# A selective-scan network on one core: the loads of delta * u in a different split and order

## The chip, the cores and the metric

The kernel runs on one core of one Trainium2 chip. The time is device microseconds of one execution, from three runs, of which the median counts. One further execution was taken by the hardware profiler; every row, wait and timeline below comes from it.

## What is computed

The network has four layers over a batch of 4 images of 64 x 64 pixels and 96 channels. Layers 0 and 1 are selective-scan (Mamba) layers and take most of the time; layers 2 and 3 are linear attention with a small quantised feed-forward part. A scan layer expands to 192 channels, applies a 3 x 3 convolution, and runs a state-space recurrence along four directions of the image (rows, columns, and both reversed). Its core, for every image, direction, channel and 16 states, over 4096 positions, is

```
dA = exp(delta * A)
h  = dA * h + delta * u * B        # u: the convolved input
y  = sum over the 16 states of h * C
```

after which the four directions are added, normalised, gated and projected.

## The kernel before

The two scan layers work on the images in pairs, so there are four phases (2 layers x 2 pairs). A phase first prepares (`prepare`): normalisation, convolution, `delta`, and the product `delta * u`, which go to DRAM; the end of the previous phase (`finish`) is woven into it. Then comes the scan stage (`scan_phase`), which is written out by hand, with the order of every engine's instructions fixed.

In the scan stage the 128 partitions hold 8 groups (4 directions x 2 images) x 16 states. Of these, partition p belongs to group (p / 4) mod 8, so each quarter of 32 partitions holds all 8 groups with 4 of the states. The work is cut into 128 units: 8 chunks of 512 positions, and in each chunk 16 blocks of 12 channels. One unit is a tile `h` of 128 partitions x 12 channels x 512 positions, f32. For each unit:

- SP loads the tile `dlt` (delta in three bf16 parts, 24 partitions, line 376), and into `h` the product `delta * u` (line 396). DRAM holds that product for the 8 groups, in two equal copies; each row of it goes to four partitions.
- GpSimd multiplies `h` by B in place, three channels at a time (`times_b`, line 406), half a unit ahead of the scans.
- TensorE spreads `dlt` over the partitions into PSUM (`replicate`, line 412), ScalarE makes `exp` of it (`decay`, line 416), and VectorE does the recurrence, one scan of 512 positions for each channel (`scan`, line 423). From chunk 1 on the scans start from the carry of the chunk before.
- One unit later TensorE multiplies by C (`contract`, line 441), ScalarE evicts (line 453), and SP stores `y` in four transfers (line 461).

There are four `h` buffers. `load(units[at + 3])` is written after the last scan of unit `at` and after the stores of unit `at - 1`, and so three units ahead; a chunk's B and C are loaded by four transfers each at the ends of blocks 8 and 15. All these transfers are in SP's queue in that order. The transfers in SP's queue use eight completion semaphores in turn, so each one waits until the eighth-last has landed.

`load_quarters(u, e, n, first, quarters)` loads `n` channels from channel `e` into `quarters` quarters from quarter `first` on: 32 partitions from one copy of `delta * u`, or 64 partitions from both. One packet is one partition's 6 channels, 12,288 bytes. The order in which `load` calls it is a tuple and an inner loop over the two halves of the channels:

```
        n = EB // 2
        for first, quarters in ((1, 2), (0, 1), (3, 1)):
            for e in range(0, EB, n):
                self.load_quarters(u, e, n, first, quarters)
```

Of the kernel before, what the change touches and what calls it, by code (L numbers as in the profile page):

```python
# [32 lines left out]
EB = 12  # L33
# [47 lines left out]
class Consts:  # L81
# [3 lines left out]
    def load(self, pool, name, shape):  # L85
        t = pool.tile(shape, F32, name=name)
        self.nc.sync.dma_start(t, self.a[name])
        return t
# [39 lines left out]
class Scans:  # L128
# [19 lines left out]
    def prepare(self, ph):  # L148
# [16 lines left out]
        with self.tc.tile_pool(name="prep", bufs=1) as wp, self.tc.tile_pool(  # L165
# [3 lines left out]
            def load(name, shape, at=0):  # L169
                t = wp.tile([at + shape[0]] + shape[1:], F32, name=name)  # L170
                nc.sync.dma_start(t[at:], a[pre + name])
                return t

            xp = load("x_proj", [C, 2, 2, XD2])
            dt_w = load("dt_w", [XD2 - 2 * NS, 2, E], at=2 * NS)
            conv_b = load("conv_b", [C, 2])
            ds = load("Ds", [C, 2, K])
            dsum = wp.tile([C, 2], F32, name="dsum")
# [202 lines left out]
    def load(self, u):  # L381

        nc, ph = self.nc, u.ph
        u.h = self.units.tile([128, EB, TC], F32, name="h", bufs=4)
        self.load_delta(u)
        n = EB // 2
        for first, quarters in ((1, 2), (0, 1), (3, 1)):
            for e in range(0, EB, n):
                self.load_quarters(u, e, n, first, quarters)

    def load_quarters(self, u, e, n, first, quarters):

# [591 lines left out]
```

## Time and profile before

| | us |
|---|---|
| median of three runs (lowest, highest) | 12483.71 (12462.94, 12492.15) |
| the profiled execution's own time | 12443.48 |
| its span, first to last instruction | 12441.7 |
| scan stages, four | 1909, 1911, 1912, 1929 |
| before the first scan; the three preparations between the stages; after the last scan | 774; 923, 932, 926; 1201 |
| busy: TensorE, VectorE, GpSimd, ScalarE | 10107.0, 9376.9, 7386.0, 7185.6 |
| loads of `h`: transfers, size | 2048 of 384 KB (32 partitions), 1024 of 768 KB (64 partitions) |

PE is TensorE's matmuls, PEld its weight loads, DVE VectorE, ACT ScalarE, POOL GpSimd, SP SyncE; a q after the name is that engine's queue. A row of the page gives the line, engine, operation, tiles (out<-in), shape and count, then busy time and mean ns of one, then the engine's idle time before it and what ended most of it. Rows of digits are tenths of busy time in 40 equal slices of the span. The row of DMA is the mean over 16 DMA engines: 0.5 there can mean that eight of them are full. Timeline rows give the start, the length, and in brackets the idle time before and what ended it.

### The profile page before, as it was taken

Reading aid. Unit: us, or ns where it says so; the run is one execution under the profiler, and the core shown is the slowest. Engines: PE = TensorE matmul, PEld = TensorE weight load, DVE = VectorE, ACT = ScalarE, POOL = GpSimd, SP = SyncE. Lnnn points to the kernel's source line nnn. Section 1 sums busy time; section 2 is a strip of 40 time slices with the busy share of each in tenths; the row PEclk is TensorE's granted clock in tenths of the full one; section 3 lists DMA queues with packets and bytes.
Section 4 is the critical chain, followed back from the end, with each engine's and each line's share of the span. In section 5 each row is a group of like instructions: output and inputs, shape, how many; then the busy total and the mean of one; then the engine's idle time right before and its main releaser. Section 6 shows DMA issues by size and latency. Waiting matters only on the chain.

```text
span 12441.7 us, 340858 instructions
## 1 busy us (share of the span) xinstructions
PE 10107.0 (81%) x147008; PEld 4972.1 (40%) x147008; DVE 9376.9 (75%) x9235; ACT 7185.6 (58%) x11815; POOL 7386.0 (59%) x2316
## 2 busy tenths in 40 slices
PE   7758888879878888879878888888878888887777
PEld 2224444433334444433334444443334444444333
DVE  2479999963569999982469999992459999993567
ACT  2456666644456666653456666663446666662556
POOL 0159999950149998960139899880129989990000
PEclk8665565669675555659775656558776655557787
DMA  3567676754667676764566777664567666663110
GB/s 92 172 227 247 244 248 247 248 168 140 213 205 246 245 247 244 250 200 128 176 215 244 246 247 249 243 226 125 174 202 249 244 243 245 245 244 122 30 21 11
DMA packets 882704, 2491.45 MB, mean 200 GB/s; under 512 B 279058, under 2 KB 561840, under 8 KB 737456
## 3 DMA queue, kind: packets, MB, share of 16 engines
q1 hardware_dynamic: 552496, 2163.38, 50.6%
q10 hardware_dynamic: 328704, 306.26, 8.5%
q8 instruction: 1158, 18.97, 0.7%
q14 instruction: 346, 2.83, 0.1%
HBM read 1955.42 MB, written 513.80 MB: 198 GB/s over the span
## 4 chain that ended last, share of the span: by engine, by line
DMA 53%; PE 20%; SPq 8%; DVE 7%; ACT 4%; issue 4%; POOL 3%; ACTq 1%; POOLq 0%; DVEq 0%
DMA h<-du 47%; PE c L260 8%; SPq L396 7%; POOL h L406 3%; PE f L591 2%; DVE h L423 2%; PE d L306 2%; DMA yk<-y 1%; PE c L289 1%; PE f L600 1%; POOL parts L320 1%; PE f L682 1%; DMA du<-du_sb 1%; PE y L441 1%; DVE parts L321 1%
## 5 line engine op out<-in xcount | busy, mean ns | idle before, releaser
L406 POOL TENSOR_TENSOR h<-h,b 128x1536 f32<-128x1536 f32 x2048 | 7016.6, 3456 | 780.6 <-DMA h<-du 369.0
L423 DVE TENSOR_TENSOR_SCAN h<-a,carry,h 128x512 f32<-128x512 f32 x5376 | 6356.7, 1259 | 391.8 <-POOL h L406 360.9
L416 ACT ACTIVATE a<-a,a_col 128x512 f32<-128x512 f32 x6144 | 4030.3, 662 | 1966.6 <-PE a L412 1814.4
L441 PEld LDWEIGHTS y<-h,cw 128*32 128x32 f32 x131072 | 2886.3, 145 | 3597.6 <-issue 1606.1
L441 PE MATMUL y<-h,cw 128*32 128x48 f32 x131072 | 3702.1, 269 | 438.0 <-ACT a L416 216.9
L412 PE MATMUL a<-dlt,rep 24*128 24x512 bf16 x6144 | 3319.4, 551 | 884.8 <-DVE h L423 782.1
L320 POOL CAST parts<-dl 96x1024 bf16<-96x1024 f32 x256 | 341.3, 1348 | 3092.1 <-DVE dl L317 2785.6
L316 DVE TENSOR_TENSOR du_sb<-dl,xc 96x1024 f32<-96x1024 f32 x256 | 397.3, 1577 | 1296.2 <-ACT dl L314 1234.8
L453 ACT COPY d<-y 128x384 f32<-128x384 f32 x2048 | 979.6, 478 | 485.7 <-PE y L441 432.7
L260 PE MATMUL c<-xn,taps 96*96 96x512 f32 x2304 | 1034.1, 609 | 73.5 <-DVE xn L245 71.0
L423 DVE TENSOR_TENSOR_SCAN h<-a,h 128x512 f32<-128x512 f32 x768 | 869.6, 1201 | 189.0 <-ACT a L416 110.6
L412 PEld LDWEIGHTS <-rep 24*128 24x128 bf16 x6144 | 471.9, 101 | 903.6 <-issue 451.0
L306 PE MATMUL d<-xd,dt_w 7*96 7x512 f32 x1024 | 520.8, 859 | 254.9 <-ACT xd L292 225.6
L260 PEld LDWEIGHTS c<-xn,taps 96*96 96x96 f32 x2304 | 382.6, 167 | 707.5 <-issue 628.7
L823 POOL MEMSET tn<- 1x4096 f32 x8 | 27.8, 3506 | 865.0 <-PE pa L843 514.7
L267 ACT ACTIVATE xc<-c,conv_b 96x512 f32<-96x512 f32 x128 | 87.3, 682 | 718.1 <-PE c L260 633.2
L591 PE MATMUL f<-yk,perm 128*128 128x384 f32 x1024 | 415.9, 546 | 99.6 <-DMA yk<-y 88.8
L314 ACT ACTIVATE dl<-d 96x1024 f32<-96x1024 f32 x256 | 252.0, 1017 | 400.9 <-DMA delta<-parts 234.5
L321 DVE TENSOR_TENSOR parts<-dl,parts 96x1024 bf16<-96x1024 f32 x256 | 366.9, 1455 | 153.2 <-POOL parts L320 153.1
L289 PE MATMUL c<-xc,x_proj 96*103 96x512 f32 x512 | 420.2, 958 | 4.2 <-ACT xc L267 4.2
L306 PEld LDWEIGHTS d<-xd,dt_w 7*96 7x96 f32 x1024 | 151.7, 212 | 542.4 <-ACT xd L292 295.8
L360 ACT ACTIVATE cw<-c,gmask 128x256 f32<-128x256 f32 x512 | 287.9, 573 | 126.2 <-DMA h<-du 65.9
(114 smaller groups left out, 5650.6 us busy)
## 6 DMA issues: line engine op xcount, KB each, us to landing
h<-du SPq DMA_DIRECT2D x1024, 768.0 KB
h<-du SPq DMA_DIRECT2D x2048, 384.0 KB
delta<-parts ACTq DMA_DIRECT2D x512, 288.0 KB
dlt<-delta SPq DMA_DIRECT2D x512, 288.0 KB
du<-du_sb SPq DMA_DIRECT2D x256, 384.0 KB
du<-du_sb ACTq DMA_DIRECT2D x256, 384.0 KB
y<-d SPq DMA_DIRECT2D x2048, 48.0 KB
yk<-y SPq DMA_DIRECT2D x256, 384.0 KB
```

Of the source, the lines that this page charges most:

```text
L260: nc.tensor.matmul(rows(ps[:C]), taps[:, tap, h * C : (h + 1) * C], xn[:, ROWS * c + dy : ROWS * (c + 1) + dy, dx : dx + HW], start=tap == ...
L289: nc.tensor.matmul(rows(ps[:XD2]), xp[:, k, h], u[:, h], start=h == 0, stop=h == 1)
L306: nc.tensor.matmul(ps[:, m], dt_w[part, k, m * C : (m + 1) * C], xd[part], start=True, stop=True)
L321: nc.vector.tensor_tensor(parts[:, 2], delta, parts[:, 1], ALU.subtract)
L396: self.nc.sync.dma_start(u.h[32 * first : 32 * (first + quarters), e : e + n].rearrange("p e t -> p (e t)"), source.rearrange("a g e t -> ...
L406: self.nc.gpsimd.tensor_tensor(h, h, b, ALU.mult)
L412: self.nc.tensor.matmul(u.a[n], rep, u.dl[:, n], start=True, stop=True)
L416: self.nc.scalar.activation(u.a[n], u.a[n], AF.Exp, scale=u.ph.a_col[:, at : at + 1])
L423: self.nc.vector.tensor_tensor_scan(u.h[:, n], u.a.pop(n), u.h[:, n], 0.0 if u.c == 0 else u.ph.carry[:, at : at + 1], ALU.mult, ALU.add,)
L441: self.nc.tensor.matmul(view(u.y[32 * j : 32 * j + 32], l2 * EB, (8 * EB, 4), (1, EB)), u.ph.cw[u.c][:, l1, 8 * j + l2], view(u.h, 64 * l1 ...
L453: self.nc.scalar.copy(u.d[:, :, :, l1], u.y[:, : 32 * EB].rearrange("p (t h x) -> p t h x", t=4, h=2))
L591: nc.tensor.matmul(ps[:, : 4 * C].rearrange("p (w v e) -> p w v e", w=4, v=nv), cst.perm[:, k], view(t, off, (sw if k < 2 else -sw, 4), (1 ...
```

## The change

The three kinds of transfer, each made for channels 0 to 5 and for channels 6 to 11, were the middle half (partitions 32 to 95), quarter 0 (0 to 31) and quarter 3 (96 to 127): six transfers. Channels 6 to 11 keep these three. Channels 0 to 5 come in two halves instead: 64 to 127 and 0 to 63. The order is now

1. channels 6 to 11, partitions 32 to 95
2. channels 6 to 11, partitions 0 to 31
3. channels 0 to 5, partitions 64 to 127
4. channels 0 to 5, partitions 0 to 63
5. channels 6 to 11, partitions 96 to 127

`load_quarters`, the data and the rest of the kernel are unchanged.

```diff
--- before.py
+++ after.py
@@ -384,9 +384,8 @@
         u.h = self.units.tile([128, EB, TC], F32, name="h", bufs=4)
         self.load_delta(u)
         n = EB // 2
-        for first, quarters in ((1, 2), (0, 1), (3, 1)):
-            for e in range(0, EB, n):
-                self.load_quarters(u, e, n, first, quarters)
+        for first, quarters, e in ((1, 2, n), (0, 1, n), (2, 2, 0), (0, 2, 0), (3, 1, n)):
+            self.load_quarters(u, e, n, first, quarters)
 
     def load_quarters(self, u, e, n, first, quarters):
 
```

## The prediction

> **What bounds the kernel now.** I read the page first, then the busy times by stage, then the waits and the timeline of one unit, then the records of single transfers. From the page:
>
> ```profile
> span 12441.7 us, 340858 instructions
> ...
> DVE  2479999963569999982469999992459999993567
> ...
> DMA  3567676754667676764566777664567666663110
> ...
> DMA 53%; PE 20%; SPq 8%; DVE 7%; ACT 4%; issue 4%; POOL 3%; ACTq 1%; POOLq 0%; DVEq 0%
> ...
> L406 POOL TENSOR_TENSOR h<-h,b 128x1536 f32<-128x1536 f32 x2048 | 7016.6, 3456 | 780.6 <-DMA h<-du 369.0
> L423 DVE TENSOR_TENSOR_SCAN h<-a,carry,h 128x512 f32<-128x512 f32 x5376 | 6356.7, 1259 | 391.8 <-POOL h L406 360.9
> ```
>
> VectorE shows four plateaus of nines, the scan stages. There it is nearly full, and what idle time it has ends with GpSimd's multiply, which itself waits for `h<-du`. The DMA row stands at 6 to 7 tenths, and yet DMA leads the chain. The stages, with columns PE, PEld, DVE, ACT, POOL busy, clock, DMA share, GB/s:
>
> ```profile
> 775.00:2684.00 1909.00, 1621.64 (x34042) 832.57 (x34041) 1805.52 (x1536) 1305.54 (x2268) 1740.52 (x508) 0.60 0.70 245
> 3613.00:5524.00 1911.00, 1624.24 (x34042) 833.32 (x34041) 1806.32 (x1536) 1306.72 (x2269) 1740.56 (x509) 0.60 0.70 244
> 6462.00:8374.00 1912.00, 1625.12 (x34042) 832.86 (x34041) 1806.35 (x1536) 1307.18 (x2268) 1740.75 (x508) 0.60 0.70 244
> 9306.00:11235.00 1929.00, 1626.64 (x34042) 833.21 (x34041) 1807.04 (x1536) 1308.57 (x2268) 1740.52 (x508) 0.60 0.69 242
> ```
>
> Stage time less VectorE busy is 103.5 + 104.7 + 105.7 + 122.0 = 436 us: all that faster loads can give while VectorE does the same scans. Where it sits, from the timeline (VectorE, then GpSimd):
>
> ```profile
> 1510.77 4.78 DVE L423 TENSOR_TENSOR_SCAN h<-a,carry,h 128x512 f32<-128x512 f32 x4
> 1519.54 14.21 DVE L423 TENSOR_TENSOR_SCAN h<-a,carry,h 128x512 f32<-128x512 f32 x12 [3.98 <-POOL h L406]
> ```
>
> ```profile
> 1516.06 13.66 POOL L406 TENSOR_TENSOR h<-h,b 128x1536 f32<-128x1536 f32 x4 [4.48 <-DMA h<-du]
> ```
>
> A unit's twelve scans run without a gap; the stall stands before the first. From the scan starts: scans 1 to 11 of a unit follow each other at 1.177 us (chunks 1 to 7), scan 0 follows after 2.07. A unit takes 15.05 us where VectorE needs 12 x 1.177 = 14.12.
>
> **Why DMA bounds at 0.70.** A 64-partition load is written by 16 engines, four packets of 12,288 B each; a 32-partition load by eight. The trace shows this in the completion counts: the 64-partition load issued at 1513.73 has eight engines landing at 1519.3 to 1519.6 and the other eight at 1521.4 to 1522.8, and every 32-partition load has only eight late completions. So one half of the engines, 0 to 7, has six blocks of four packets a unit, and the other two. Busy times around the stall:
>
> ```profile
> 1516.50:1520.50 4.00, 1.54 (x41) 0.91 (x34) 0.96 (x1) 1.14 (x2) 4.00 (x2) 0.50 1.04 273
> 1520.50:1521.50 1.00, 0.58 (x1) 0.10 (x1) 1.00 (x2) 0.01 (x1) 1.00 (x1) 0.50 0.77 315
> 1521.50:1529.50 8.00, 7.04 (x135) 3.28 (x134) 8.00 (x8) 5.61 (x10) 8.00 (x3) 0.50 0.55 221
> ```
>
> From 1521.5 on half of the engines work, at 221 GB/s, each packet in 0.46 us. In the first stretch all sixteen work and bring only 273 GB/s: packets take 0.6 to 0.95 us there, on both halves. At 1521, again with sixteen at work, packets take 0.46 to 0.47. So two halves can run at full pace or slow each other down, depending on what they write. Engines 0 to 7 never rest: their unit is 6 blocks x 1.85 us (landings 1540.0, 1541.8, 1543.7) = 11.1, the delta tile 1.56, the four y stores 1.2, sum 13.9; the rest of the 15.05, 1.1 us, is lost while both halves are active.
>
> [...]
>
> **The change part by part.** It issues five loads for six: 4 x 128 = 512 units, 512 fewer issues of 0.645 us on SP's queue, which is not on the path once it stops waiting for its eighth-last transfer; 0. Bytes stay. Blocks on engines 0 to 7 go from 6 to 5, on 8 to 15 from 2 to 3. So engines 0 to 7 need 5 x 1.85 + 1.56 + 1.2 = 12.0 us a unit, plus a loss c while both halves work. VectorE's 14.12 is reached at c = 2.1, today's 15.05 at c = 3.05.
>
> No row shows c, so both ends: 0[...]; 3 x 1.85 = 5.55 if each block of engines 8 to 15 collides in full. By today's rate (1.1 us for two blocks) three cost 1.65. By hand from the issue order: engines 0 to 7 spend about 1.5 us on the delta tile first, so they lag not one block but 1.75. Engines 8 to 15 then do halves 32-95, 64-127, 0-63 at 0.7, 2.5, 4.4 us[...]. With some loss beside the delta tile c is 1.1 to 1.8. I take 1.65: 13.65 us, under VectorE's 14.12. GpSimd needs four multiplies at 3.41 us start to start = 13.66; TensorE in three channels 3 x 0.53 + 2 x 0.84 = 3.27 of 3.53 us at clock 0.50, and units without a stall already run so. VectorE becomes the bound.
>
> Order: channels 0 to 5 are complete after the fourth load instead of the fifth[...]. A load is issued at the end of the unit three before its own, and GpSimd must start on it some 24 us later, so about 9 us of lead covers the 4 to 5 us that eight small loads of b and c add in a chunk, as long as a unit's DMA work stays under 14.12; without that cover the stalls return.
>
> Sum: of 436 us, chunk 0 keeps about 3 us a stage, since GpSimd (13.66) is slower there than the scans without carry (12 x 1.128 = 13.54) and starts level: 12. Because the margin is only 0.5 us a unit I leave a tenth of the rest, 40. Saved: 436 - 12 - 40 = 384. The profiled execution, 12443.5 with 1.8 outside its span, would be 12060; the median of the runs is 40 above it, 12483.7, so 12483.7 - 384 = 12100.
>
> **Rivals.**
> Partial gain: c is 2.1 to 3.05, engines 0 to 7 still bound. For: 1.65 is near 2.1, and a backlog makes the next middle half meet the last quarter, as today. Against: the hand schedule. At 14.6 us a unit, 448 units x 0.45 = 200 saved: 12280.
> Slower: the halves fall into step, so that two of engines 8 to 15's blocks collide in full (c = 3.7, beyond the 3.05 where it decides). A unit takes 15.7 us: 448 x 0.65 + 64 x (15.7 - 14.1) = 290 + 100, 12870. For: packets on both halves already double in places, and a transfer waits for the eighth-last one, which ties both halves together. Against: the extra 1.85 us block that is gone, and the packets at 0.46 with sixteen engines.
> Hidden anyway, no change: would need c at 3.05 by chance, or SP's issue as the bound; against the latter, SP waits for loads 502 us of the first scan stage.
> The 64-partition loads not spreading over 16 engines is excluded: they have the shape of today's.
>
> **How the numbers follow.** VectorE bound, 12100, 12030 to 12160: 0.64. Partial, up to 12455: 0.22. Within 0.2% (25 us, about what a measurement of this kernel can tell from no change): 0.04. Slower: 0.10. The low end is the ceiling, 12483.7 - 436, with the runs' spread of 20; up to 12330 takes in most of the partial cases.
>
> **What would show it.** Right: scan stages of 1810 to 1825 us, VectorE busy still 1806; scan 0 following at under 1.4 us; the `h<-du` wait of GpSimd nearly gone; SP waiting for compute more than for transfers; late completions 16, 8, 16, 16, 8 a unit. DMA share stays near 0.7 with GB/s near 258. Wrong: packets near 0.92 us with sixteen engines most of the time, and stages of 1900 or more.

## The result: 4.5% slower

The changed kernel takes 13026.23 us (median of 4 runs, 12980.17 to 13108.25) against 12480.49 of the kernel before beside it: a ratio of 1.0446, 95% interval 1.039 to 1.0501. The forecast was 12100 us, with a range of 12030 to 12330. The profiled execution has a span of 13009.0 us against 12441.7.

The page of the changed kernel, the lines that answer to those shown of before (line numbers are one lower from here on, since the diff takes a line away):

```profile
span 13009.0 us, 339405 instructions
...
DVE  2478888872568888882468988883458898884566
...
DMA  3578888864678878874568878884568888885110
...
DMA 57%; PE 20%; DVE 7%; SPq 6%; ACT 4%; issue 3%; POOL 3%; ACTq 1%; POOLq 0%; DVEq 0%
...
L405 POOL TENSOR_TENSOR h<-h,b 128x1536 f32<-128x1536 f32 x2048 | 7010.6, 3454 | 1359.6 <-DMA h<-du 786.5
L422 DVE TENSOR_TENSOR_SCAN h<-a,carry,h 128x512 f32<-128x512 f32 x5376 | 6361.9, 1260 | 889.0 <-POOL h L405 851.6
```

The work is the same, 3454 ns a multiply and 1260 ns a scan. What grew is the chain of waits that bounded before: GpSimd for the loads (369 to 787 us), VectorE for GpSimd (361 to 852). DMA engines are busier, mostly 8 tenths for 6 to 7. By stage (PE, PEld, DVE, ACT, POOL busy, clock, DMA share, GB/s):

```profile
775.00:2857.00 2082.00, 1668.34 (x34042) 846.47 (x34041) 1808.33 (x1537) 1312.91 (x2269) 1738.54 (x508) 0.55 0.81 225
3790.00:5821.00 2031.00, 1635.16 (x34042) 842.83 (x34041) 1807.21 (x1536) 1300.10 (x2268) 1739.75 (x508) 0.59 0.81 230
6752.00:8809.00 2057.00, 1673.72 (x34088) 848.31 (x34090) 1807.71 (x1536) 1311.33 (x2265) 1739.05 (x508) 0.55 0.81 227
9739.00:11804.00 2065.00, 1658.99 (x34042) 845.47 (x34041) 1806.74 (x1536) 1307.72 (x2268) 1738.93 (x508) 0.56 0.81 226
```

The four stages together are 574 us longer (8235 against 7661), which is all of the span's 567; preparations and tail are as before. VectorE's busy time has not moved. The DMA engines are busy for a larger share (0.81 for 0.70) and move less in that time (227 GB/s for 244): the same bytes at a slower pace. In the transfer records a packet of 12,288 B takes 0.70 us on average, 0.55 before; 36% take over 0.8 us, 9% before. A unit takes 15.9 to 16.7 us in chunks 1 to 7 (means by chunk over the four stages), and the stall sits where it sat, before scan 0 (first row VectorE, second GpSimd):

```profile
4223.26 14.21 DVE L422 TENSOR_TENSOR_SCAN h<-a,carry,h 128x512 f32<-128x512 f32 x12 [2.81 <-POOL h L405]
```

```profile
4219.77 13.65 POOL L405 TENSOR_TENSOR h<-h,b 128x1536 f32<-128x1536 f32 x4 [3.36 <-DMA h<-du]
```

Why packets are slow shows in six microseconds of that unit, with all sixteen engines busy:

```profile
4225.00:4231.00 6.00, 5.21 (x102) 2.45 (x100) 6.00 (x6) 3.91 (x7) 6.00 (x3) 0.50 1.02 232
```

A share of 1.02 and 232 GB/s is little more than what eight engines brought alone in the kernel before (221). In the same stretch the completion counts of the third load (64 to 127) show all sixteen engines landing together, from 4227.96 to 4229.38 but for one straggler at 4233.86, and the fourth (0 to 63) likewise from 4231.47 to 4232.87, with one at 4237.19. All do the same transfer at the same time, into one half of the partitions; packets there take 0.91 us in the median. The planned distance, one half of the engines a block ahead of the other, is not there.

### The profile page after: what moved, and what is told of

Its sections match the earlier page's. It is cut to its first block, busy times and chain, and to the rows that moved or that the text cites. A ratio compares the mean times of both kernels' runs of the same rounds, so it can differ in the third digit from the quotient of the medians.

```text
span 13009.0 us, 339405 instructions
## 1 busy us (share of the span) xinstructions
PE 10247.0 (79%) x147008; PEld 5025.3 (39%) x147008; DVE 9382.0 (72%) x9235; ACT 7191.8 (55%) x11815; POOL 7380.9 (57%) x2316
## 4 chain that ended last, share of the span: by engine, by line
DMA 57%; PE 20%; DVE 7%; SPq 6%; ACT 4%; issue 3%; POOL 3%; ACTq 1%; POOLq 0%; DVEq 0%
DMA h<-du 52%; PE c L260 8%; SPq L395 5%; DVE h L422 3%; POOL h L405 2%; PE f L590 2%; PE d L306 2%; DMA yk<-y 1%; PE y L440 1%; PE c L289 1%; PE f L599 1%; PE f L670 1%; POOL parts L320 1%; DMA delta<-parts 1%; PE f L681 1%
## 5 line engine op out<-in xcount | busy, mean ns | idle before, releaser
L405 POOL TENSOR_TENSOR h<-h,b 128x1536 f32<-128x1536 f32 x2048 | 7010.6, 3454 | 1359.6 <-DMA h<-du 786.5
L422 DVE TENSOR_TENSOR_SCAN h<-a,carry,h 128x512 f32<-128x512 f32 x5376 | 6361.9, 1260 | 889.0 <-POOL h L405 851.6
L440 PEld LDWEIGHTS y<-h,cw 128*32 128x32 f32 x131072 | 2922.2, 146 | 3780.2 <-issue 1915.3
L411 PE MATMUL a<-dlt,rep 24*128 24x512 bf16 x6144 | 3396.2, 568 | 1184.3 <-DVE h L422 1087.6
L440 PE MATMUL y<-h,cw 128*32 128x48 f32 x131072 | 3768.1, 269 | 575.3 <-issue 267.5
```

The lines of the kernel that those rows point to most:

```text
L405: self.nc.gpsimd.tensor_tensor(h, h, b, ALU.mult)
L411: self.nc.tensor.matmul(u.a[n], rep, u.dl[:, n], start=True, stop=True)
L422: self.nc.vector.tensor_tensor_scan(u.h[:, n], u.a.pop(n), u.h[:, n], 0.0 if u.c == 0 else u.ph.carry[:, at : at + 1], ALU.mult, ALU.add,)
L440: self.nc.tensor.matmul(view(u.y[32 * j : 32 * j + 32], l2 * EB, (8 * EB, 4), (1, EB)), u.ph.cw[u.c][:, l1, 8 * j + l2], view(u.h, 64 * l1 ...
```

## Where a unit's 16.2 us go

Completion counts tell when the engines finished each load: in both traces every 64-partition load has sixteen late ones, every 32-partition load and every delta tile eight. They carry no engine number; engines 0 to 7 is here a name for the eight of the 32-partition loads. That these are always the same eight is read from the kernel before: its four such loads issued from 1518.66 to 1520.83 land one after the other, from 1525.07, 1526.91, 1528.76 and 1530.70 on, 1.84 to 1.94 us apart, while the DMA share is 0.55. Of sixteen landings the earlier eight are taken for engines 8 to 15 and the later eight for 0 to 7; where all sixteen land close together, this overstates the distance. The end of a load is the median of the eight landings less 0.5 us, the time from the last packet to the landing where the traces show eight engines then falling silent (in the kernel before, packets up to about 1521.5 and landings from 1521.95 on). A transfer is taken to start at the earliest 1.4 us after its issue, as measured with the transfers alone below. So the time of engines 0 to 7 can be cut by what they do, and by what 8 to 15 do meanwhile; means over chunks 1 to 6 of the first two phases, us a unit:

```
engines 0-7:        delta   1st    2nd    3rd    4th    5th    y     nothing   sum
assumed              1.56   1.85   1.85   1.85   1.85   1.85   1.2      -      12.0
measured             1.96   2.26   2.29   3.42   2.74   1.89   0.90    0.72    16.2
both halves in the third load 1.82 us (median packet 0.92); both in the fourth 1.51 (0.93);
0-7 in the third while 8-15 in the fourth 1.5 (0.77)
```

The loss c is 4.2 us a unit. Third and fourth load take 2.5 of it, the first two and the delta tile about 1.2, and for 0.7 us engines 0 to 7 have nothing to do. (The forecast of a run below names 3.16 for the third load, an earlier estimate from the same landings; 3.42 is the count with the 0.5 us that the traces show.)

What they wait for is SP. Five loads leave its queue in 7.57 us, not in 5 x 0.65; six took 7.75 in the kernel before (second row):

```profile
4217.12 7.57 SPq L395 DMA_DIRECT2D h<-du  x5
```

```profile
1513.73 7.75 SPq L396 DMA_DIRECT2D h<-du  x6
```

In the first stage SP waits 579 us at the loads of `h` (502 before) and 313 us at the delta tile (140 before) for earlier transfers (the changed kernel, then the kernel before; waited for: us, times, longest):

```profile
SPq L395 <- DMA h<-du: 578.9, 331, 4.0
SPq L376 <- DMA h<-du: 313.1, 112, 3.3
```

```profile
SPq L396 <- DMA h<-du: 502.4, 330, 4.0
SPq L376 <- DMA h<-du: 140.2, 111, 2.8
```

In both traces the transfers name eight semaphores in turn (100 to 107), and in every unit all late landings of a load come before the next issue on its semaphore. A unit has ten transfers on SP, so the third load must wait until the fifth load of the unit before has landed on its last engine: in 89% of the units it is issued within 0.05 us after that landing. From issue of the first to issue of the third it takes 5.0 us in the median. The units of this one trace differ in this, and can be sorted by it (medians):

```
issue 1st -> 3rd load   units   8-15 ahead of 0-7 at the third   0-7: end of 2nd to end of 4th
under 2 us                56              2.8 us                          4.6 us
4 to 5                   187              2.2                             5.9
5 to 6                   132              0.95                            7.2
6 to 7                   126              0.64                            8.0
```

Seven units lie outside these rows. Two blocks at 0.46 us a packet are 3.7 us, at 0.92 they are 7.4. Where the third load goes out at once the planned distance is there and nearly free; where it goes out late, engines 0 to 7 have caught up by the time it comes, both halves begin it together, and the fourth stays in step. The sorting alone does not tell which comes first, since slow loads also land late and so hold up the next issue; the experiments have to.

## Experiments

Two theories stand against each other: **same side** (packets are slow while both halves of the engines write on one side of partition 64, and late issue puts them in step) and **sixteen at once** (packets are slow whenever all sixteen work). Inside the first, the **delta tile's lag** stands against the **late third load** as what spoils the distance. Each result below is given in us, with its ratio to the kernel before and the 95% interval of the ratio. Some edits are shown shortened.

### The transfers alone

```
+        for first, parts, lines in ((32, 64, 16), (0, 64, 16), (64, 64, 16), (0, 32, 8), (0, 128, 16), (0, 128, 32)):
+            for _ in range(4):
+                nc.sync.dma_start(t[first : first + parts], x as [lines][parts // lines, step 0][6 * TC])
```

> The kernel before with 24 extra transfers ahead of everything else, four each of six kinds, from the input x, one after the other into one tile: 64 partitions from partition 32, from 0, from 64; 32 partitions from 0; 128 partitions from 16 lines given to 8 partitions each; 128 partitions from 32 lines given to 4 each. Packets are 12,288 B as in the loads of h. [...] about 0.46 us a packet for 64 from 32 and for 32 from 0, about 0.93 for 64 from 0 and 64 from 64. Rate theory (sixteen engines at once are slow whatever they write): the three kinds of 64 partitions alike. Both leave the 128-partition kinds open[...]; that decides whether such a load can serve the scan stages. Total: about 100 to 200 us over before.

Measured: 12637.25 us in all, one execution; from the transfer records, per transfer, for those that ran by themselves:

```
partitions   lines   median packet us   first packet to last, us
32 to 95      16          0.46              3.2
0 to 63       16          0.92 to 0.93      4.5
64 to 127     16          0.89 to 0.91      4.4
0 to 31        8          0.46              2.8
0 to 127      16          0.87 to 0.94      8.2
0 to 127      32          0.46              5.0
```

The two 128-partition kinds inside their transfers, no compute engine working (columns as in the stages):

```profile
106.70:114.20 7.50, 0.00 (x0) 0.00 (x0) 0.00 (x0) 0.00 (x0) 0.00 (x0) 1.00 0.94 203
134.10:138.20 4.10, 0.00 (x0) 0.00 (x0) 0.00 (x0) 0.00 (x0) 0.00 (x0) 1.00 0.97 354
```

Sixteen engines at once are not slow: they bring 354 GB/s at 0.46 us a packet. In the 64-partition kinds nothing but the partitions differs, and they decide: 0.46 us for those on both sides of 64, 0.89 to 0.93 for those on one side. Two transfers that fill the same 128 partitions from 16 or from 32 lines differ by a factor of 1.7 in GB/s; no record tells why. Once a load of 0 to 63 and one of 64 to 127 were in the queue together: the two took 7.7 us from first packet to last, at 0.885 us a packet. That is near the 7.4 of eight packets an engine at 0.92, not the 3.7 at 0.46: started in step, the two loads gain little from writing different sides.

### Delta tile last

```
-        self.load_delta(u)
         n = EB // 2
         for first, quarters, e in (...):
             self.load_quarters(u, e, n, first, quarters)
+        self.load_delta(u)
```

> The changed kernel with the load of the delta tile moved behind the five loads of h, so that engines 0 to 7 start each unit level with 8 to 15 and not 1.5 us late. If the lag of the delta tile is what spoils the one-block distance (the step of my hand schedule that lost 1.1 us a unit), the loss falls and the time is 12100 to 12600. If the distance is lost elsewhere, because the third load comes so late that both halves of the engines start it together, it stays at 12900 to 13150.

Measured 13325.65 us, 1.0698 (1.0641 to 1.0754), outside both ranges. Taking the lag away costs another 300 us. The third load goes out 6.1 us after the first in the median, the halves are 0.46 us apart where that is 6 to 7 us (248 units of 508), and third and fourth load take 8.0 us there. The lag does not spoil the distance; it is part of what is left of it. Not all of the 300 us need be the lag's: here the fourth load also waits, for the delta tile of the unit before, in 89% of the units within 0.05 us of its landing.

### y stores from ScalarE's queue

```
-            self.nc.sync.dma_start(
+            self.nc.scalar.dma_start(
                 u.ph.y[row : row + 4, :, b, :, u.eb].rearrange("j g h x -> (j g) h x"),
```

> The changed kernel with the four y stores of a unit issued from ScalarE's queue, so that SP's queue carries six transfers a unit and its eighth-last lies a whole unit back: the third load waits for the first load of the unit before, no longer for its fifth. If that wait makes both halves of the engines start the third and fourth load together, the loss falls: 12100 to 12700. [...] 12900 to 13150. If issuing on ScalarE costs (four issues of some 0.4 us a unit on an engine with 3.5 us to spare), it is hidden.

Measured 13424.64 us, 1.0769 (1.0751 to 1.0787), again outside both ranges, but the inside is as the late-load theory wants it: the third load goes out 1.35 us after the first in the median, and in 405 of 508 units, where that is under 2 us, engines 8 to 15 are 2.7 us ahead and third and fourth load take 4.4 us. The total is worse for another reason. The eight semaphores turned out to be shared by both queues (in the traces of the kernel before and the changed one, too, SP's and ScalarE's transfers name the same 100 to 107), so ScalarE now waits with its `exp` behind a store, and SP behind ScalarE's stores (engine, line, waited for: us, times, longest):

```profile
ACT a L415 <- DMA y<-d: 1314.3, 467, 4.8
```

```profile
SPq L376 <- DMA y<-d: 3474.5, 390, 13.5
```

By the count used above, engines 0 to 7 have nothing to do for 3.7 us of a 17 us unit. So the total says nothing on the distance, and the load times do.

### The two sides exchanged

```
-        for first, quarters, e in ((1, 2, n), (0, 1, n), (2, 2, 0), (0, 2, 0), (3, 1, n)):
+        for first, quarters, e in ((1, 2, n), (3, 1, n), (0, 2, 0), (2, 2, 0), (0, 1, n)):
```

> The changed kernel[...]: second load quarter 3, third 0 to 63, fourth 64 to 127, fifth quarter 0. [...] 0.5 to 1.5 us more a unit if the lag is the 1.75 blocks of that schedule: 13250 to 13800. If instead both halves of the engines start the third load together, because its issue waits for the fifth load of the unit before[...]: 12900 to 13150.

Measured 12972.38 us, 1.0421 (1.0397 to 1.0444), like the changed kernel. Both halves are in the third load together for 1.56 us a unit and in the fourth for 1.35. Where the halves are in step, which side comes first makes no difference (1.0421 for 1.0446); my hand schedule would have had it slower.

### The same packets on every engine, in a load of 128 partitions

```
-            self.dram.tile([2, G, E + PITCH, TC], F32, name="du", bufs=2 * NC) for _ in range(NC)
+            self.dram.tile([4, G, E + PITCH, TC], F32, name="du", bufs=2 * NC) for _ in range(NC)
-                queue.dma_start(ph.du[cc][copy, g, :E].rearrange("(h e) t -> e h t", h=2), du)
+                for a in (2 * copy, 2 * copy + 1):
+                    queue.dma_start(ph.du[cc][a, g, :E].rearrange("(h e) t -> e h t", h=2), du)
-        for first, quarters, e in ((1, 2, n), (0, 1, n), (2, 2, 0), (0, 2, 0), (3, 1, n)):
+        for first, quarters, e in ((1, 2, n), (0, 1, n), (0, 4, 0), (3, 1, n)):
-        copies = slice(0, 2) if quarters == 2 else slice(first % 2, first % 2 + 1)
+        copies = slice(0, quarters) if quarters > 1 else slice(first % 2, first % 2 + 1)
```

> The changed kernel with its third and fourth load (channels 0 to 5, partitions 64 to 127 and 0 to 63) as one load of all 128 partitions from 32 lines, which ran alone at 0.46 us a packet; delta * u is stored in four copies for it, so two more stores of 384 KB for each of 256 blocks of the preparations. Each engine gets the same packets as in the changed kernel (20 and 12 a unit). [...] the third and fourth load lose the 2.2 us that they take over 2 x 1.85 (3.16 + 2.73 on engines 0 to 7),[...] VectorE becomes the bound: scan stages of 1800 to 1840 us. If sixteen engines at once are slow[...], or the eight semaphores alone do it, the stages stay at 2000 to 2080. The preparations get longer by what the stores add, 0 to 200 us each; the stages decide.

Measured 12524.4 us, 1.0064 (1.0049 to 1.0079) of before. The stages answer the question (two of the four):

```profile
913.00:2706.00 1793.00, 1467.40 (x34042) 813.49 (x34041) 1792.69 (x1536) 1275.49 (x2269) 1739.68 (x509) 0.83 0.73 260
3781.00:5574.00 1793.00, 1457.40 (x34042) 812.33 (x34041) 1792.79 (x1536) 1273.84 (x2269) 1740.54 (x509) 0.85 0.73 260
```

VectorE is busy for 1792.7 of 1793 us: nearly every stall is gone, and scan 0 follows at 1.174 us. Engines 0 to 7 carry 20 packets of `h` a unit and 8 to 15 carry 12, exactly as in the changed kernel, all sixteen work at once, at 260 GB/s. This is the gain that I forecast for five blocks, and some 20 us a stage more: GpSimd did not hold chunk 0 back (13.37 us a unit there), and VectorE's own busy time fell by 13 us.

The run has one transfer fewer a unit, but the eight semaphores are still there: its third load waits for the last load of the unit before, as in the changed kernel. Yet it goes out 1.39 us after the first in the median, for 5.0, because that load has landed by then. In the first stage SP waits 47.5 us at the loads of `h`, for 578.9, and mostly for ScalarE:

```profile
SPq L461 <- ACT a L416: 832.9, 113, 12.0
SPq L396 <- DMA h<-du: 47.5, 41, 3.3
```

So the eight semaphores alone do not make the third load late. Slow packets and late issue feed each other: loads at 0.9 us a packet land late, late landings hold up the third load (5.0 us after the first), and a late third load lets both halves start it together. A load that ran alone at 0.46 us in place of the two breaks this circle. The late issue is older than the change: the third load of the kernel before already goes out 4.6 us after the first.

With both channel halves as such loads (`for first, quarters, e in ((0, 4, 0), (0, 4, n))`):

> As the run with one load of 128 partitions, and channels 6 to 11 as a second such load in place of the remaining three: two loads a unit, 16 packets on every engine. [...] engines 0 to 7 need 2 x 3.7 + 1.8 + 1.2 = 10.4 us a unit, so VectorE bounds, scan stages of 1800 to 1825 us and less waiting than with the half. If the loads share the rate of all sixteen engines, 1900 to 2080. With preparations as before the total would be 12100; each extra us of the four preparations adds to it.

12506.07 us, 1.0046 (1.003 to 1.0063), stages again 1793 us. The remaining loads were no longer a bound, so nothing is added.

### The price of the copies

The kernel before stores the four copies, with its loads unchanged.

> The kernel before with the two extra stores of delta * u alone, loads unchanged: the price of the copies. 512 stores of 384 KB are 201 MB; at 230 GB/s that is 0.22 ms of each preparation's transfers, where DMA is busy 0.54 of 925 us, so it may be hidden: 0 to 200 us on each of four preparations, 12480 to 13280, scan stages unchanged at 1910 to 1930.

Measured 13043.53 us, 1.048 (1.0459 to 1.0501). The stages take 1916 to 1928 us; from the last scan of a stage to the first of the next it is 1071 to 1084 us for 930 to 940, and 920 for 775 before the first. The price is not hidden: about 143 us for each preparation, more than the 116 to 135 that a stage gains.

### A version that beats both

If engines 0 to 7 need 15.05 us with six loads and about 10.4 with 128 partitions (the estimate in the forecast above), only some units have to be fast, and only their channels need four copies. To the kernel before (with room for four copies, and `copies` as above):

```
+            for copy in (2, 3):
+                nc.sync.dma_start(
+                    ph.du[cc][copy, g, :E].rearrange("(h e) t -> e h t", h=2)[:48], du[:48]
+                )
-        for first, quarters in ((1, 2), (0, 1), (3, 1)):
+        fast = u.eb % 8 < 4
+        for first, quarters in ((0, 4),) if fast else ((1, 2), (0, 1), (3, 1)):
```

> The kernel before, with loads of 128 partitions (two a unit) in the units of blocks 0 to 3 and 8 to 11 of a chunk, the six loads in the others; delta * u of those channels alone is stored in two more copies (two stores of 192 KB more for each block of the preparations, SP's queue). Engines 0 to 7 then need about 10.4 and 15.05 us in turns of four units, 12.7 on average, and four slow units use up 3.8 us of a lead of about 9. [...] scan stages of 1792 to 1805 us. The copies cost half of what they cost for all channels, so 60 to 80 us for each preparation, or less because ScalarE no longer issues any of them. Together 12449 - 4 x (118 - 70) = 12260, 12200 to 12330.

12342.91 us, 0.9915 (0.99 to 0.9929), just outside the range: stages of 1793 to 1797 us, but the copies cost 85 to 95 us between stages and 120 before the first, more than I gave them.

With a quarter of the units (`[:24]`, `u.eb % 8 < 2`):

> The same for blocks 0, 1, 8 and 9 alone: a quarter of the units, 13.9 us on average on engines 0 to 7, against 14.1 of VectorE; six slow units in a row use up 5.7 us of the lead. [...] scan stages of 1792 to 1830 us, as the balance is nearly even. The extra copies (96 KB each[...]) cost 30 to 60 us for each preparation: 12449 - 4 x (105 - 40) = 12190, 12100 to 12330.

12217.92 us, 0.9817 (0.9801 to 0.9834), the best of all. Two of its stages:

```profile
807.00:2628.00 1821.00, 1462.71 (x34042) 813.41 (x34041) 1798.65 (x1536) 1273.87 (x2269) 1738.15 (x508) 0.84 0.73 256
3591.00:5425.00 1834.00, 1460.99 (x34046) 812.68 (x34049) 1799.49 (x1537) 1274.93 (x2269) 1739.15 (x508) 0.85 0.73 254
```

Some 20 to 35 us of stall a stage stay, the copies cost about 33 us for each preparation, and the total is 230 us lower, of the 436 that there were to win.

## Why the prediction was wrong, point by point

- **The bound.** Right: engines 0 to 7 bound the scan stages through GpSimd, with the stall before scan 0. The loads of 128 partitions turned 1909 us into 1793, so the ceiling of 436 us was, if anything, low (the four stages give 489).
- **The bookkeeping of blocks.** Right: six blocks to five, 20 packets instead of 24. With c near 2 the same load gives a stage without a stall. The lead of about 9 us was my estimate.
- **The step that failed** is "512 fewer issues of 0.645 us on SP's queue, which is not on the path once it stops waiting for its eighth-last transfer; 0", and the hand schedule built on it, with loads starting on engines 8 to 15 at 0.7, 2.5 and 4.4 us. SP never stopped waiting. The third load goes out 5.0 us after the first, not 1.3, and the distance of 1.75 blocks shrinks to half a block or less in half of the units. c was taken as 1.1 to 1.8, an estimate whose loss of 1.1 us in one meeting of the two halves no trace had shown, and is 4.2. The trace of the kernel before had it: there too the third load goes out 4.6 us after the first in the median (1518.66 after 1513.73 in the unit of the timeline), held up by the last load of the unit before, which is its eighth-last in both kernels.
- **The other estimate of c**, three blocks at today's rate, failed as well: today's two blocks of engines 8 to 15 belong to loads of 32 to 95, which ran alone at 0.46 us a packet; of the new three, two belong to loads of 64 to 127 and 0 to 63, which ran alone at 0.89 to 0.93. A loss per block can't be carried over to a transfer of another shape. Nor was today's 1.1 us all lost while both halves work: by the count above, about 0.5 of it is time in which engines 0 to 7 have nothing to do. They never rest in the unit that was read, but they do in the mean.
- **The rival "slower"** named what happened: the halves in step, held together by the wait for the eighth-last. It was priced at c = 3.7 and 12870, and measured at 4.2 and 13026. That the two are close is partly luck: the two blocks lose 2.5 us in the mean, not 3.7, as not all units are fully in step, and the rest of c lies in the first two loads, the delta tile and the 0.7 us without work, which it did not price. I gave it one chance in ten although its "for" listed the very wait that the sum of the change put at zero.
- **The packets at 0.46 with sixteen engines**, which the prediction holds against the halves in step, are no such case: the loads at work at 1521 are two of 32 to 95, which run at 0.46 alone as well. Loads of 0 to 63 and of 64 to 127 did run mostly side by side in the 56 units with early issue (4.6 us for third and fourth load), and less so in the others (5.9 to 8.0).
- **What would show it wrong** was stated as packets near 0.92 us most of the time and stages of 1900 or more; the stages are there, and the packets in a third of all cases.

Open is the straggler. In the changed kernel the last engine lands 1.4 to 2.2 us behind the last but one in the median, depending on the load, and over 4 us behind in 13 to 34% of the loads (before 0.5 to 1.2, and over 4 us in 1.4% at most). Since a load counts as landed with its last engine, this one engine makes most of SP's wait: the third load waits 2.1 us in the mean after the issue of the second has ended, and would wait 0.6 if the last landing came with the one before it and all else stayed (an estimate from the landings). In the unit shown it goes out at 4222.67; the last engine landed at 4222.65, the one before it at 4219.33. The delay goes with packets at half pace: it is 0.2 to 0.3 us in the run with one load of 128 partitions in place of the two, 0.1 to 0.5 with the stores on ScalarE, and 3.0 to 4.7 with the delta tile last. But a single load at half pace does not bring it about: with the transfers alone it is at most 0.3. What keeps one engine back, no run here tells. Nor was the wait for the eighth-last taken away by itself: moving the stores took the same semaphores along.

## What to carry to other kernels

A schedule in which two groups of DMA engines stay a block apart is only as good as the issue that feeds it: count the transfers that may be in flight and ask which one each issue waits for, before taking issue as free. Where a transfer is slow by its shape, change the shape instead of looking for an order in which it should not matter: one load of 128 partitions from 32 lines (0.46 us a packet) in place of two of 64 (about 0.9) took 238 to 289 us out of each scan stage here, and exchanging the two did not help (1.0421 for 1.0446). And where a bound is an average over units, making only a quarter of them fast can bring most of the gain, at a quarter of the price.

## What the runs showed of the hardware

- A 64-partition load on sixteen engines takes 0.46 us a packet of 12,288 B on partitions 32 to 95, 0.89 to 0.93 on 0 to 63 or 64 to 127.
- A 128-partition load on sixteen engines takes 0.46 us a packet (354 GB/s) from 32 source lines of 4 partitions each, and about 0.9 (203 GB/s) from 16 lines of 8 each.
- Loads at half pace in a busy queue go with one late engine: the last landing comes 1.4 to 2.2 us behind the last but one in the median in the changed kernel, 0.2 to 0.3 us in the run with one load of 128 partitions in place of the two.
- In this kernel SP's and ScalarE's transfers take turns on the same eight completion semaphores (100 to 107 in both traces), and with the stores on ScalarE's queue its `exp` waited 1314 us for them in all.
